# A normalised causal-attention layer on one NeuronCore: the store and the gather of the next batch's statistics registered one visit earlier

## The chip, the cores and the metric

The kernel runs on one core of one Trainium2 chip. A core has a matrix engine (PE, its weight loads shown as PEld), a vector engine (DVE), an activation engine (ACT), a general engine (POOL) and a sequencer (SP) that here only issues transfers. Each engine works through its own queue in order; between engines there are semaphores alone. The metric is the time of one execution on the device, in microseconds (us), lower is better. Times stand as the median of several runs; one more execution was taken with the profiler, and all views come from that one.

## The reference

The input x has 32 batches of 256 channels by 32x32 pixels (1024 tokens), in float32. Each batch is normalised in groups of eight channels, projected to queries, keys and values for eight heads of 32 channels, and put through attention in which a token sees only the tokens strictly before it; the result is added to x.

```python
g = x.reshape(B, 32, 8, H, W)                       # 32 groups of 8 channels
xn = (g - mean(g, axis=(2, 3, 4))) / sqrt(var(g, axis=(2, 3, 4)) + 1e-5)
q  = q_w @ xn + q_b;   k, v = split(kv_w @ xn + kv_b)
scores = q.T @ k / sqrt(32)                         # per head, 1024 x 1024
scores = where(mask == 0, -10000, scores)           # mask: strictly lower triangle
attn = where(mask == 0, 0, softmax(scores))
return x + attn @ v
```

## The kernel before

**Tiling.** Two groups of four heads (index g) and five blocks of keys and queries per group make ten *visits* per batch (N = 10, `VISITS`, line 692). In visit i the kernel forms scores on PE (`scores`, line 437) into the PSUM tiles `sT` and `tri`, takes exponentials on ACT (lines 473 and 476) into the tiles `e` and `eh`, and lets POOL zero what lies above the diagonal (`mask`, line 416, through `select`, line 411). One visit later PE multiplies the masked exponentials with the values (`values`, line 491, matmuls of line 502 into `acc`), ACT copies a finished `acc` into a tile `num` (line 511), and DVE adds exponentials up over keys (line 521), which gives the softmax's denominators. So PE, ACT, POOL and DVE work on neighbouring visits, and there are 320 visits in all.

**Order of the work.** It is written out by hand: `tc.manual_schedule` keeps every engine's instructions in the order in which Python emits them. The loop at line 881 goes through the visits; in visit i it emits, in this order, the scores, exponentials and masks of visit i; the first part of the products of visit i-1; whatever the table `at` holds for i; the second part of the products; DVE's additions of visit i-1, mixed with the chains in the table `beside`; and last whatever the table `after` holds for i. The function `when` (line 754) fills these tables, and tuples such as `PROJECT`, `PREPARE`, `SUMS`, `STACK`, `FINISH` give the visit of each step relative to the first visit of its batch (`first + n`).

**Statistics of a later batch.** `prepare` (line 757) registers twelve steps for batch b, at the visits `first + PREPARE[k]`:

- k = 0, 1: `norm_channels`, four `bn_stats` on DVE (line 195) that write the tile `st`, spread between DVE's additions.
- k = 2: `norm_gather`, one DMA issued by SP (line 207) that stores `st` (12 KB) to the DRAM tile `each`.
- k = 3: `norm_spread`, one indirect DMA issued by POOL (line 214) that reads `each` back so that every partition holds the numbers of all eight channels of its group, in the tile `eight`. It waits for the store.
- k = 4: `norm_groups`, two `bn_aggr` on DVE (line 223) from `eight` to `mv`, and two small operations (lines 224, 225).
- k = 5: `norm_rstd`, two operations on POOL (lines 252, 256): the power -0.5, and the shift.
- k = 6 to 11: `norm_apply`, which writes the normalised input `xn` on ACT (line 271) for the projections (line 179).

**What else stands around it.** On POOL: two transfers per denominator, which fold the sums `e` from 128 to 64 and from 64 to 32 rows (`fold`, line 550). On SP: the transfers `folded<-e` that put the four folded sums under each other (line 556), the store and the spread of the inverses (lines 616, 630: `rb<-inverses`), the outputs (line 662) and the input of two batches ahead (line 115). On DVE, for the batch two back: `num<-num,rb` (line 668) and `rb<-num,v_bias_col,x` (line 659), which is the last reader of a `num` tile, so that ACT may write it anew.

Of the kernel before, what the change touches and what calls it, by code (L numbers as in the profile page):

```python
# [33 lines left out]
def tile_norm_attention_residual(  # L34
# [69 lines left out]
    def unshifted():  # L104
# [652 lines left out]
        def prepare(b, whens):  # L757
            for n, f in zip(whens, [
                lambda: norm_channels(b, 0), lambda: norm_channels(b, 1), lambda: norm_gather(b), lambda: norm_spread(b),
                lambda: norm_groups(b), lambda: norm_rstd(b),  # L760
            ] + [lambda hf=hf, g=g: norm_apply(b, hf, g) for hf, g in ((0, 0), (0, 1))]
              + [lambda g=g, s=s: norm_apply(b, 1, g, (s,)) for g in range(NG) for s in range(2)]):
                if n is None:
                    in_turn([f() or []])
                elif isinstance(n, tuple):
                    n[1].setdefault(n[0], []).insert(len(beside.get(n[0], ())) if n[1] is beside else 0, f)
                else:
                    when(n, f, after)
# [8 lines left out]


        PROJECT = (-5, -4, -4, -3, -2, -1, 0, 1, 1, 2, 3, 4)
        PREPARE = (-13, -12, -10, -10, -9, -8, -7, -6, -5, -4, -4, -3)  # L780
        SUMS = (4, 6, 9, 11)
        STACK = (6, 9, 12, 14)
        LOAD = 5
# [5 lines left out]
        with tc.manual_schedule(engines={ENG.PE, ENG.Activation, ENG.DVE, ENG.Pool, ENG.SP}):  # L789
# [47 lines left out]
            for b in range(B):  # L837
# [4 lines left out]
                if b >= 2:  # L842
                    for n in range(NG * NH):
# [5 lines left out]
                    prepare(b, [  # L849
                        (first + n, {5: at}.get(k, beside)) if k in (0, 1, 4, 5) else first + n for k, n in enumerate(PREPARE)  # L850
                    ])
# [60 lines left out]
    def shifted():  # L912


        with ExitStack() as inner:
# [34 lines left out]
            with tc.For_i(0, B, 1) as b:  # L950
# [93 lines left out]
                )  # L1044

    inside = unshifted()
    ALL = 3 * P * ROW
    held = nc.values_load(
# [29 lines left out]
```

## Time and profile before

| what | value |
|---|---|
| median of the runs (lowest to highest) | 1793.87 us (1793.67 to 1795.77) |
| the profiled execution's own time | 1794.61 us |
| its span, first to last instruction | 1792.9 us |
| mean granted clock of PE over the span | 0.999 |
| busy: PE, DVE, ACT, POOL | 1763.3, 1598.2, 1450.1, 1195.0 us |
| busy share: PE, DVE, ACT, POOL | 98%, 89%, 81%, 67% |

The span is divided into 32 batches of some 55 us. "Busy" counts an engine's own instructions; issuing a DMA from SP, waits and branches are not counted. In a timeline a row gives the start (us from the span's start), the duration, engine, line, operation, output<-inputs, the count of merged instructions, and in brackets the idle time before the row with what ended it. In the list of waits a row gives who waited for what: total us, number of times, longest. In the chain of waits each row is one step of the chain that ended last, with its start and duration. A wait for several semaphores is put down to the one that came last.

### The profile page before, as it was taken

The numbers are of one execution on the slowest core, as the hardware profiler recorded it, in microseconds if no ns is written. First come the engines' busy times: TensorE is split into PE (matmuls) and PEld (weight loads), VectorE is DVE, ScalarE is ACT, GpSimd is POOL, SyncE is SP. The second block draws the span as 40 slices with busy tenths as digits, with TensorE's granted clock in tenths as the row PEclk, the third lists the DMA queues.
The fourth block names the chain that finished last, engine by engine and source line by source line (L and its number), as shares of the span: only waits on it lengthen the run. The fifth ranks groups of instructions, "written<-read, shape, count | busy, mean of one in ns | idle before, by whom it ended". The sixth has DMA issues, their size and how long they took to land.

```text
span 1792.9 us, 82114 instructions
## 1 busy us (share of the span) xinstructions
PE 1763.3 (98%) x37144; PEld 1074.1 (60%) x37144; DVE 1598.2 (89%) x1668; ACT 1450.1 (81%) x1736; POOL 1195.0 (67%) x1191
## 2 busy tenths in 40 slices
PE   9999999999999999999999999999999999999997
PEld 6666556556565565565655666656656656666564
DVE  4698888988889898898899999889999999999998
ACT  6888877888878877788888888778888888888885
POOL 2567766677666676666767667756677776677662
PEclk9999999999999999999999999999999999999999
DMA  2566767676666766667676677766777776767663
GB/s 69 99 121 142 145 123 139 141 142 138 131 144 133 140 137 135 138 136 146 137 141 129 138 147 141 145 120 138 149 141 140 144 131 135 150 142 145 131 127 89
DMA packets 92772, 240.23 MB, mean 134 GB/s; under 512 B 26272, under 2 KB 27792, under 8 KB 76544
## 3 DMA queue, kind: packets, MB, share of 16 engines
q0 software_dynamic: 17360, 100.58, 39.6%
q1 hardware_dynamic: 74912, 134.28, 26.3%
q8 instruction: 291, 4.77, 1.1%
q14 instruction: 65, 0.53, 0.1%
q10 hardware_dynamic: 144, 0.07, 0.0%
HBM read 69.90 MB, written 34.95 MB: 58 GB/s over the span
## 4 chain that ended last, share of the span: by engine, by line
PE 84%; DMA 6%; DVE 4%; ACT 3%; issue 1%; POOL 1%; SPq 0%; POOLq 0%; ACTq 0%; DVEq 0%
PE acc L502 25%; PE pp L179 21%; PE tri L404 13%; PE sT L404 13%; PE ppv L179 12%; DMA eight<-each,group_of 5%; DVE e L521 2%; ACT eh L476 1%; DVE rb L659 1%; ACT e L473 1%; ACT num L511 0%; POOL e L550 0%; DMA wn<-in_L_conv_kv_w_dram 0%; DMA rb<-inverses 0%; DMA folded<-e 0%
## 5 line engine op out<-in xcount | busy, mean ns | idle before, releaser
L473 ACT ACTIVATE e<-sT 128x1024 f32<-128x1024 f32 x640 | 621.1, 1023 | 198.5 <-PE sT L404 191.5
L404 PE MATMUL sT<-q,k 32*64 32x512 f32 (+3 forms) x6144 | 534.0, 522 | 0.0
L404 PE MATMUL tri<-q,k 32*64 32x64 f32 (+5 forms) x10752 | 522.7, 313 | 10.4 <-ACT eh L476 10.3
L404 PEld LDWEIGHTS tri<-q,k 32*64 32x64 f32 x10752 | 377.2, 130 | 191.7 <-issue 72.9
L179 PE MATMUL pp<-xn,wT 128*32 128x256 f32 x8192 | 490.8, 379 | 0.7 <-issue 0.7
L521 DVE TENSOR_TENSOR e<-e,eh 128x1536 f32<-128x1536 f32 x315 | 444.1, 1410 | 32.4 <-PE acc L502 24.5
L476 ACT ACTIVATE eh<-tri 128x1536 f32<-128x1536 f32 (+1 forms) x320 | 439.1, 1372 | 27.5 <-DVE e L521 18.1
L521 DVE TENSOR_TENSOR e<-e,e 128x2048 f32<-128x2048 f32 x189 | 453.7, 2400 | 3.3
L411 POOL TENSOR_SCALAR_AFFINE_SELECT diagonal<-eh 128x256 f32<-128x256 f32 (+1 forms) x384 | 400.4, 1218 | 21.2 <-ACT eh L476 17.7
L179 PEld LDWEIGHTS pp<-xn,wT 128*32 128x32 f32 x8192 | 262.6, 110 | 229.7 <-ACT e L473 61.9
L550 POOL DMA_DIRECT2D e<-e x248 | 256.3, 1034 | 182.2 <-DMA e<-e 103.7
L502 PE MATMUL acc<-e,v 128*32 128x512 f32 x2560 | 339.5, 600 | 8.3 <-ACT num L511 8.1
L404 PEld LDWEIGHTS sT<-q,k 32*64 32x64 f32 x6144 | 268.0, 131 | 8.4 <-ACT k L286 4.1
L179 PE MATMUL ppv<-wT,xn 128*32 128x256 f32 x4096 | 247.2, 381 | 0.3 <-issue 0.3
L502 PE MATMUL acc<-eh,v 128*32 128x384 f32 (+1 forms) x2560 | 199.9, 403 | 0.0
L411 POOL TENSOR_SCALAR_AFFINE_SELECT corner<-e 128x256 f32<-128x256 f32 x64 | 64.5, 1009 | 199.8 <-ACT e L473 199.8
L521 DVE TENSOR_TENSOR e<-e,diagonal 128x1024 f32<-128x1024 f32 x126 | 182.2, 1446 | 7.4 <-POOL corner L425 0.5
L179 PEld LDWEIGHTS ppv<-wT,xn 128*32 128x32 f32 x4096 | 126.6, 110 | 90.2 <-ACT e L473 16.5
L411 POOL TENSOR_SCALAR_AFFINE_SELECT e<-e 128x512 f32<-128x512 f32 x64 | 142.2, 2223 | 4.4
L223 DVE BATCH_NORM_AGGREGATE mv<-eight 128x2 f32<-128x96 f32 x62 | 35.9, 582 | 119.4 <-DMA eight<-each,group_of 119.4
L271 ACT ACTIVATE xn<-x,shift,rstd 128x256 f32<-128x256 f32 x248 | 138.6, 596 | 0.0
L502 PEld LDWEIGHTS acc<-eh,v 128*32 128x32 f32 x2560 | 76.6, 110 | 90.9 <-issue 64.0
(99 smaller groups left out, 1578.1 us busy)
## 6 DMA issues: line engine op xcount, KB each, us to landing
e<-e POOLq DMA_DIRECT2D x124, 512.0 KB, 6.0
x<-in_x_dram SPq DMA_DIRECT2D x124, 256.0 KB, 4.2
e<-e POOLq DMA_DIRECT2D x124, 256.0 KB, 4.8
folded<-e SPq DMA_DIRECT2D x124, 256.0 KB, 5.6
rb<-inverses SPq DMA_DIRECT2D x124, 256.0 KB, 4.0
out_dram<-rb SPq DMA_DIRECT2D x124, 256.0 KB, 5.3
x<-in_x_dram SPq DMA_DIRECT2D x2, 512.0 KB, 4.7
inverses<-inv_turned SPq DMA_DIRECT2D x31, 32.0 KB, 2.9
```

The source lines that it names most:

```text
L179: nc.tensor.matmul(out[part], lhsT=lhsT[:, part], rhs=rhs, start=start, stop=stop, skip_group_check=True)
L223: return [lambda g=g: nc.vector.bn_aggr(mv[:, g, :], live["eight", b][:, :, g, :]) for g in range(NG)] + [lambda: nc.vector.tensor_scalar( ...
L271: nc.scalar.activation(to, of, AF.Identity, bias=live["shift", b][:, g : g + 1], scale=rstd)
L404: return nc.tensor.matmul(to, lhsT=live["k", b, g][rows, kb * P + c : kb * P + c + KEYS], rhs=of, start=True, stop=True, skip_group_check=True
L411: nc.gpsimd.affine_select(out=to, in_=of, pattern=[[0, 4], [1, to.shape[-1]]], compare_op=ALU.is_gt, fill=0.0, base=first - (P - 1 if odd ...
L473: nc.scalar.activation(e[:, heads[a][0] : heads[a][1] + 1 : step, :], banks[a], AF.Exp)
L476: exp = nc.scalar.activation(eh[:, :, :wide], tri.rearrange("p (j q) -> p j q", q=SHORT)[:, :, :wide], AF.Exp)
L502: nc.tensor.matmul(acc[HD * j : HD * (j + 1), of], lhsT=live["v", b][:, kb, h * HD : (h + 1) * HD], rhs=e[:, j, :], start=first, stop=last ...
L521: nc.vector.tensor_add(to, to, tile_of(b, g, at))
L550: nc.gpsimd.dma_start(out=total[:rows], in_=total[rows : 2 * rows], accum_op=ALU.add)
L659: nc.vector.scalar_tensor_tensor(rb, num, v_bias_col[:, g : g + 1], xt[:, g, cols], ALU.add, ALU.add)
```

## The change

One number of the tuple `PREPARE` is changed twice: steps k = 2 (the store by SP) and k = 3 (the gather by POOL) of every batch from the third on are registered 11 instead of 10 visits before the batch's first visit. That is visit 9 of the batch two ahead of it, instead of visit 0 of the batch just ahead of it. Both steps stay in the table `after`, so they are emitted last in their visit.

```diff
         PROJECT = (-5, -4, -4, -3, -2, -1, 0, 1, 1, 2, 3, 4)
-        PREPARE = (-13, -12, -10, -10, -9, -8, -7, -6, -5, -4, -4, -3)
+        PREPARE = (-13, -12, -11, -11, -9, -8, -7, -6, -5, -4, -4, -3)
```

POOL's queue before, around visit 0 of batch 14. Names: `e_1_0` is the sum of group 1, first half of the queries, of batch 13; `corner`, `e_0_0`, `eh_0_0` are tiles of visit 0 of batch 14; `diagonal_0_1` of its visit 1; `eight` and `each` hold the statistics for batch 15.

```order
L550 DMA e_1_0_12082<-e_1_0_12082 64x2048
L411 AFFINE_SELECT corner_0_12558<-e_0_0_12520 128x4x64
L411 AFFINE_SELECT e_0_0_12520<-e_0_0_12520 128x4x128
L424 MEMSET e_0_0_12520 1x4
L425 COPY corner_0_12558<-eh_0_0_12521 64x4x64
L411 AFFINE_SELECT eh_0_0_12521<-eh_0_0_12521 128x4x128
L550 DMA e_1_0_12082<-e_1_0_12082 32x2048
L214 DMA eight_12611<-each_12609,group_of 128x192
L411 AFFINE_SELECT diagonal_0_1_12653<-eh_0_1_12614 128x4x128
L411 AFFINE_SELECT diagonal_0_1_12653<-eh_0_1_12614 128x4x64 x2
```

POOL's queue with the change, at the same place:

```order
L550 DMA e_1_0_12082<-e_1_0_12082 64x2048
L214 DMA eight_12522<-each_12520,group_of 128x192
L411 AFFINE_SELECT corner_0_12562<-e_0_0_12524 128x4x64
L411 AFFINE_SELECT e_0_0_12524<-e_0_0_12524 128x4x128
L424 MEMSET e_0_0_12524 1x4
L425 COPY corner_0_12562<-eh_0_0_12525 64x4x64
L411 AFFINE_SELECT eh_0_0_12525<-eh_0_0_12525 128x4x128
L550 DMA e_1_0_12082<-e_1_0_12082 32x2048
L411 AFFINE_SELECT diagonal_0_1_12653<-eh_0_1_12614 128x4x128
L411 AFFINE_SELECT diagonal_0_1_12653<-eh_0_1_12614 128x4x64 x2
```

The gather has moved ahead of six rows: the five operations that mask visit 0, and the second fold of `e_1_0`. It now stands behind the first fold of `e_1_0`.

SP's queue with the change, at the same place (`folded` gathers batch 13's sums, `rb` and `inverses` belong to batch 12):

```order
L616 DMA inverses_12338<-inv_turned_12336 128x2x32
L630 DMA rb_12424<-inverses_12338 32x4x512 x2
L556 DMA folded_12280<-e_0_1_11744 32x2048
L207 DMA each_12520<-st_12324 128x24
L630 DMA rb_12424<-inverses_12338 32x4x512 x2
L556 DMA folded_12280<-e_1_0_12082 32x2048
```

Apart from the number of a buffer these rows stood in this order before as well: between the ends of visits 9 and 0 SP issues nothing else, so the store keeps its place. The queues of PE, ACT and DVE are unchanged too.

## The prediction

> **What bounds the kernel now.** I read the batches' lengths first, by the busy time of the engines in stretches that run from the start of one visit 0's masks to a later one's (length, then busy time and instructions of PE, PEld, DVE, ACT, POOL, then PE's granted clock, DMA share, GB/s). They hold 11, 9 and 6 batches.
>
> ```profile
> 241.94:852.94 611.00, 600.09 (x12678) 363.97 (x12672) 552.84 (x573) 497.03 (x595) 417.54 (x407) 1.00 0.69 138
> 852.94:1348.58 495.64, 491.19 (x10376) 299.18 (x10368) 454.79 (x469) 407.06 (x487) 342.57 (x334) 1.00 0.70 139
> 1348.58:1675.38 326.80, 326.25 (x6919) 199.92 (x6912) 300.78 (x313) 271.62 (x325) 232.38 (x223) 1.00 0.70 140
> ```
>
> A batch takes 611.00/11 = 55.55 us in the first stretch, 55.07 in the second, 54.47 in the third. In the third PE is busy for 326.25 of 326.80 us: that is PE's own floor at full clock. In the first it idles 10.91 us, 0.99 per batch. So PE bounds the kernel, and what can be won is the distance from 54.47.
>
> What stops PE? The waits of the first stretch, then the one that matters in the third:
>
> ```profile
> DVE mv L223 <- DMA eight<-each,group_of: 45.8, 11, 4.7
> ACT num L511 <- DVE rb L659: 14.1, 11, 1.6
> ACT eh L476 <- DVE e L521: 10.8, 11, 1.0
> PE acc L502 <- ACT num L511: 7.0, 11, 1.0
> PE tri L404 <- ACT eh L476: 3.9, 11, 0.4
> DVE num L668 <- DMA rb<-inverses: 3.7, 8, 0.8
> ```
>
> ```profile
> DVE mv L223 <- DMA eight<-each,group_of: 20.8, 6, 3.6
> ```
>
> PE's two waits are 7.0 + 3.9 = 10.9 us, all that it idles. Each happens once per batch, and the chain of waits shows where both begin (batch 14):
>
> ```profile
> 805.84 5.16 DMA eight<-each,group_of
> ...
> 811.53 0.76 DVE rb L659
> ...
> 812.38 0.59 ACT num L511
> ...
> 813.94 1.77 DVE e L521
> ...
> 815.79 1.25 ACT eh L476
> ```
>
> The gather of the next statistics lands late, DVE stands at its `bn_aggr`, behind it in DVE's queue stands the `rb` operation for which ACT waits to overwrite `num`, and PE waits for ACT to empty `acc`; the late addition `e` holds the next exponential in the same way. DVE's wait is 4.16 us per batch in the first stretch and still 3.47 in the third, where PE loses nearly nothing: the first 3.5 us of it are covered by slack, and only the rest reaches PE, through two restarts. It need not vanish to be free.
>
> **What moves.** POOL's gather passes six POOL rows; nothing moves on SP, so the store leaves when it did. POOL before, in batch 14 (visit 0's masks from 797.48 to 804.78, the gather thereafter at 805.84):
>
> ```profile
> 793.96 0.85 POOL L550 DMA_DIRECT2D e<-e  x1 [1.79 <-PE pp L179]
> 797.48 1.23 POOL L411 TENSOR_SCALAR_AFFINE_SELECT corner<-e 128x256 f32<-128x256 f32 x1 [2.68 <-ACT e L473]
> 798.78 2.03 POOL L411 TENSOR_SCALAR_AFFINE_SELECT e<-e 128x512 f32<-128x512 f32 x1
> ...
> 803.27 1.51 POOL L411 TENSOR_SCALAR_AFFINE_SELECT eh<-eh 128x512 f32<-128x512 f32 x1
> ...
> 806.96 1.38 POOL L411 TENSOR_SCALAR_AFFINE_SELECT diagonal<-eh 128x512 f32<-128x512 f32 x3
> ```
>
> The store's row, the landing of all stores, the gather's duration on POOL and its landing (minimum, median, maximum; ns, then us):
>
> ```profile
> 794.94 0.34 SPq L207 DMA_DIRECT2D each<-st  x1
> ```
>
> ```profile
> DMA to landing us min/median/max: 1.7/5.3/6.1
> ```
>
> ```profile
> L214 POOL DMA_INDIRECT eight<-each,group_of x31: 1097/1312/1601, 17.3 to 1683.7; - x31
> ...
> DMA to landing us min/median/max: 2.9/5.1/5.7
> ```
>
> *When the gather goes.* POOL is ready for it at 794.81, the store lands at 794.94 + 5.3 = 800.2. So POOL now stands for 5.4 us at the gather, with the masks queued behind it. With the 0.3 us that POOL shows between a release and a gather (805.54 to 805.84) it starts at 800.5 and ends at 801.9; it lands at 800.5 + 5.1 = 805.6, instead of 811.0.
>
> *What DVE gains.* DVE's rows before:
>
> ```profile
> 803.05 1.23 DVE L521 TENSOR_TENSOR e<-e,diagonal 128x1024 f32<-128x1024 f32 x1
> ...
> 805.25 1.31 DVE L668 TENSOR_TENSOR num<-num,rb 128x512 f32<-128x512 f32 x2
> 811.03 0.59 DVE L223 BATCH_NORM_AGGREGATE mv<-eight 128x2 f32<-128x96 f32 x1 [4.46 <-DMA eight<-each,group_of]
> ```
>
> DVE reaches the `bn_aggr` at 805.25 + 1.31 = 806.6, one us after the new landing: no wait. Bounds: with store and gather both fastest it is the same; with both slowest (6.1, 1.6 and 5.7 us) the landing is at 807.0 and the wait 0.4, far under the 3.5 that are free. The `rb` operation then ends some 4.4 us sooner; ACT needs 1.2 of that, and the next exponential 1.0.
>
> *What the masks lose.* They start at 801.9 instead of 797.48, 4.4 us late. PE reads them here (first row: masked `e`, then `eh`, then the diagonals of visit 1; the last is today's stall):
>
> ```profile
> 804.88 1.04 PE L502 MATMUL acc<-e,v 128*32 128x512 f32 x8
> 807.60 1.07 PE L502 MATMUL acc<-eh,v 128*32 128x384 f32 x16
> 810.22 0.62 PE L502 MATMUL acc<-diagonal,v 128*32 128x128 f32 x16
> 813.01 1.07 PE L502 MATMUL acc<-e,v 128*32 128x512 f32 x8 [0.57 <-ACT num L511]
> ```
>
> At their durations of today (7.3 us in all, `e` ready after 3.4) `e` would come at 805.3, `eh` at 809.2: PE late by 0.4 and 1.6 us. But a mask's duration is not fixed. Batch 0 shows the same masks while DVE idles:
>
> ```profile
> 23.90 0.42 POOL L411 TENSOR_SCALAR_AFFINE_SELECT corner<-e 128x256 f32<-128x256 f32 x1 [5.35 <-ACT e L473]
> 24.39 0.64 POOL L411 TENSOR_SCALAR_AFFINE_SELECT e<-e 128x512 f32<-128x512 f32 x1
> ...
> 25.23 0.39 POOL L425 COPY corner<-eh 64x256 f32<-64x256 f32 x1
> 25.69 0.64 POOL L411 TENSOR_SCALAR_AFFINE_SELECT eh<-eh 128x512 f32<-128x512 f32 x1
> ```
>
> From 23.90 to 26.33 that is 2.4 us in all. And batch 14's three diagonals took 1.38 us at 806.96, in DVE's wait, against 3.47 us under DVE's additions:
>
> ```profile
> 832.70 3.47 POOL L411 TENSOR_SCALAR_AFFINE_SELECT diagonal<-eh 128x512 f32<-128x512 f32 x3
> ```
>
> The Trainium skill, "SBUF — State Buffer", section "Who interferes with whom", has the rule: a DVE instruction with two SBUF inputs and a GpSimd (POOL) instruction that reads SBUF need the same port, and the one that comes second blocks until the first is done. DVE's additions are of that kind, so by the rule this change pushes the masks against whatever DVE does from 801.9 on; were those additions as dense as at 797 to 804, the sum would end as in the slow rival below. The pairs 2.4 and 7.3, 1.38 and 3.47, bear the rule out.
>
> So it matters where DVE is from 801.9 on. Freed of its wait, it runs ahead of today's times until other data stop it. The lead is at least 0 and at most the 4.46 won. Its nearest stop that I see is the last `folded` transfer, at 822.19, which lands a median 5.6 us later, 827.8, while DVE reads it at 830.78:
>
> ```profile
> 822.19 0.51 SPq L556 DMA_DIRECT2D folded<-e  x1
> ```
>
> ```profile
> 830.78 0.70 DVE L564 STREAM_TRANSPOSE turned<-folded 128x512 f32<-128x512 f32 x1
> ```
>
> That leaves up to 3.0; I take 2. Then the last addition ends at 803.05 + 1.23 - 2 = 802.3, a few small operations follow until about 803, and DVE must stand until 805.2 for the `rb` loads: SP issues them behind a wait for PE, so they do not move (DVE waits for them in 8 of 11 batches already). The masks thus have DVE's additions beside them for 0.4 us and then a nearly idle DVE: between 2.4 and some 3.5 us, ready by 805.4 at the latest, `e` by 804. PE's 804.88 and 807.60 are met. The second fold follows at 805.4 (804.7 today), the diagonals from 806.3; even at 3.47 us they end at 809.8, ahead of 810.22.
>
> What was behind the gather in POOL's queue (diagonals, folds, the power -0.5) is no longer behind it, and the power no longer waits for DVE.
>
> **The sum.** Batches at 54.47 us: 11 x 1.08 = 11.9 us from the first stretch, 9 x 0.60 = 5.4 from the second, nothing from the third. In the second there is a gap of PE with no known cause, which I leave in (0.7):
>
> ```profile
> 1174.11 0.40 PE L179 MATMUL pp<-xn,wT 128*32 128x256 f32 x1 [0.68 <-issue]
> ```
>
> The first batches and the end stay. 11.9 + 5.4 - 0.7 = 16.6 us. The profiled execution took 1794.61 us in all, so 1778.0; it was 0.7 above the median of the runs, which is within what a run varies, so I forecast 1778 us.
>
> **Rivals.**
>
> *The masks come too late (slower).* If DVE is not ahead, its additions lie beside the masks, and they take today's 7.3 us. The point from which it decides: `eh` must be masked by 807.60, 5.7 us after 801.9. At 7.3 us PE stands 1.6 us in each of some 30 batches, 48 us, against 16.6 won: 1794.6 + 48 - 16.6 = 1826 us. With the diagonals at 3.47 us on top it is up to 3 us per batch, 1868. For it: POOL really stands 5.4 us with the masks behind it. Against: removing DVE's wait is what puts DVE ahead, and each stall of PE puts it further ahead. Chance 0.15.
>
> *The stall changes its name (no change).* The gather now runs together with the `rb` loads. If these came 3.5 us later, DVE would stand at `num<-num,rb` for what it stood at `bn_aggr`, and `rb` would be no sooner: 1794 us. For it: DVE waits there already, 3.7 us in 11 batches. Against: the gather lands in 5.1 us beside a 512 KB fold today. Chance 0.10, with whatever else would eat the gain.
>
> *The change does less than it says.* Half of it is void: the store does not move, and that is in the sum. If the gather landed as late as today, nothing would be left; but it is issued 5 us sooner.
>
> **Numbers.** The forecast has 0.75; its own range is 1773 (the third stretch's last 0.1 per batch, and a second run's level) to 1786 (half the batches keep their stall). To leave out no more than 2 in 10 the range takes in the no-change rival, to 1798. A measurement of this kernel tells about 0.2% (3.6 us) from no change: faster 0.75, same 0.10, slower 0.15.
>
> **What would show it.** Right: DVE's wait at `bn_aggr` under 1 us per batch; its wait at `num<-num,rb` grown to some 2 us; POOL's gather waiting about 5 us for `each<-st`; visit 0's masks shorter than 7.3 us; PE busy for over 99% of batches 4 to 29. Wrong: PE waiting for POOL's `eh`, `e` or `diagonal`; a landing of the gather after 810; the `rb` loads later than 806.

## The result and the profile after

The changed kernel takes 1776.14 us (median of 6 runs, 1773.88 to 1779.02) beside 1793.77 us for the kernel before (6 runs, 1789.89 to 1795.77): a ratio of 0.9904 (95% interval 0.9890 to 0.9919), 17.6 us saved. The forecast was 1778. Two later comparisons of the same pair, each beside its own runs of the kernel before, gave 1769.75 us (expected at 1776 again) and 1771.69 us, ratios of 0.9868 (0.9849 to 0.9886) and 0.9873 (0.9855 to 0.9891). So the gain is 1.0 to 1.3%, and the first figure is at its lower end.

The batches first, in the changed kernel's profile: stretches of again 11, 9 and 6 batches, from the start of one visit 0's masks to that of a later one (length, then busy time and instructions of PE, PEld, DVE, ACT, POOL, then PE's clock, DMA share, GB/s).

```profile
245.96:843.83 597.87, 597.87 (x12700) 368.02 (x12697) 554.38 (x572) 498.07 (x596) 368.39 (x408) 1.00 0.70 141
843.83:1335.74 491.91, 490.75 (x10380) 302.84 (x10376) 454.43 (x468) 407.60 (x487) 302.73 (x333) 1.00 0.71 140
1335.74:1663.27 327.53, 327.51 (x6912) 201.84 (x6908) 303.39 (x312) 270.90 (x325) 199.03 (x223) 1.00 0.71 140
```

A batch now takes 54.35, 54.66 and 54.59 us, where it took 55.55, 55.07 and 54.47. PE, which idled for 10.91 us in the first stretch, idles for none of it. Of the 17.8 us by which the span shrank (1792.9 to 1775.1) the first stretch gives 611.00 - 597.87 = 13.1 and the second 495.64 - 491.91 = 3.7; the third gives 0.7 back, and the remaining 1.7 lie ahead of these stretches and behind them.

The waits of that first stretch:

```profile
POOL eight L214 <- DMA each<-st: 49.2, 9, 6.8
...
DVE num L668 <- DMA rb<-inverses: 35.2, 11, 4.6
```

DVE's wait for `eight` (45.8 us in 11 batches before) has no row any more, and neither have ACT's two waits for DVE and PE's two for ACT. In their place stand POOL at the gather, 5.5 us in each of nine batches, and DVE at the `rb` loads, 3.2 us per batch in place of 0.3. Both are new or larger, and PE waits for neither. (In the other two batches of the stretch the profile puts POOL's wait down to an addition on DVE, 8.4 us in all; there too the gather starts 0.3 us after the store has landed, as it does in every batch of this run.)

The order of one batch (12) in the timeline, PE, DVE, POOL and SP:

```profile
672.18 0.85 POOL L550 DMA_DIRECT2D e<-e  x1 [1.05 <-PE pp L179]
...
672.85 0.53 SPq L207 DMA_DIRECT2D each<-st  x1
...
678.28 1.23 DVE L521 TENSOR_TENSOR e<-e,diagonal 128x1024 f32<-128x1024 f32 x1
...
679.47 1.15 POOL L214 DMA_INDIRECT eight<-each,group_of  x1 [6.44 <-DMA each<-st]
...
680.63 0.44 POOL L411 TENSOR_SCALAR_AFFINE_SELECT corner<-e 128x256 f32<-128x256 f32 x1
...
681.83 0.10 POOL L424 MEMSET e<- 1x4 f32 x1
...
682.33 0.64 POOL L411 TENSOR_SCALAR_AFFINE_SELECT eh<-eh 128x512 f32<-128x512 f32 x1
...
684.40 1.50 DVE L668 TENSOR_TENSOR num<-num,rb 128x512 f32<-128x512 f32 x2 [4.49 <-DMA rb<-inverses]
...
685.82 0.57 DVE L223 BATCH_NORM_AGGREGATE mv<-eight 128x2 f32<-128x96 f32 x1
```

```profile
683.12 0.59 PE L502 MATMUL acc<-e,v 128*32 128x512 f32 x1
...
686.09 1.07 PE L502 MATMUL acc<-eh,v 128*32 128x384 f32 x16
```

POOL stands 6.44 us for the store. The masks run from 680.63 to 682.97, 2.34 us in all, since DVE's last addition ended at 679.51 and DVE, but for two short operations, stands until 684.40 for `rb`. The masked `e` is there at 681.93 and PE reads it at 683.12: a margin of 1.2 us. `eh` has 3.1. DVE reaches its `bn_aggr` without a wait. In this batch that is the picture of the prediction, step for step.

### The profile page after: what moved, and what is told of

Its sections match the earlier page's. It is cut to its first block, busy times and chain, and to the rows that moved or that the text cites. A ratio compares the mean times of both kernels' runs of the same rounds, so it can differ in the third digit from the quotient of the medians.

```text
span 1775.1 us, 82114 instructions
## 1 busy us (share of the span) xinstructions
PE 1761.9 (99%) x37144; PEld 1085.2 (61%) x37144; DVE 1598.8 (90%) x1668; ACT 1450.3 (82%) x1736; POOL 1053.2 (59%) x1191
## 4 chain that ended last, share of the span: by engine, by line
PE 96%; DVE 1%; DMA 1%; issue 0%; POOL 0%; SPq 0%; DVEq 0%; ACT 0%; POOLq 0%; ACTq 0%
PE acc L502 29%; PE pp L179 25%; PE tri L404 15%; PE sT L404 14%; PE ppv L179 13%; DVE e L521 0%; DMA rb<-inverses 0%; DMA wn<-in_L_conv_kv_w_dram 0%; DMA e<-e 0%; DMA x<-in_x_dram 0%; DMA folded<-e 0%; DVE num L668 0%; DVE rb L659 0%; DVE turned L564 0%; DVE rows L567 0%
## 5 line engine op out<-in xcount | busy, mean ns | idle before, releaser
L179 PE MATMUL pp<-xn,wT 128*32 128x256 f32 x8192 | 494.0, 379 | 0.0
L179 PEld LDWEIGHTS pp<-xn,wT 128*32 128x32 f32 x8192 | 268.9, 110 | 222.7 <-ACT e L473 60.5
L411 POOL TENSOR_SCALAR_AFFINE_SELECT diagonal<-eh 128x256 f32<-128x256 f32 (+1 forms) x384 | 369.1, 1110 | 24.7 <-ACT eh L476 23.2
L550 POOL DMA_DIRECT2D e<-e x248 | 222.1, 896 | 209.1 <-DMA e<-e 101.2
L502 PE MATMUL acc<-e,v 128*32 128x512 f32 x2560 | 343.5, 600 | 0.0
L179 PE MATMUL ppv<-wT,xn 128*32 128x256 f32 x4096 | 252.2, 381 | 1.2 <-issue 1.1
L668 DVE TENSOR_TENSOR num<-num,rb 128x512 f32<-128x512 f32 x124 | 116.5, 960 | 99.0 <-DMA rb<-inverses 99.0
L179 PEld LDWEIGHTS ppv<-wT,xn 128*32 128x32 f32 x4096 | 129.6, 109 | 92.3 <-ACT e L473 18.3
L521 DVE TENSOR_TENSOR e<-e,diagonal 128x1024 f32<-128x1024 f32 x126 | 165.3, 1312 | 7.4 <-DVE e L521 0.9
L214 POOL DMA_INDIRECT eight<-each,group_of x31 | 49.9, 1608 | 166.8 <-DMA each<-st 135.1
L411 POOL TENSOR_SCALAR_AFFINE_SELECT corner<-e 128x256 f32<-128x256 f32 x64 | 56.0, 875 | 146.1 <-ACT e L473 145.7
L411 POOL TENSOR_SCALAR_AFFINE_SELECT corner<-eh 128x256 f32<-128x256 f32 x64 | 60.1, 940 | 132.3 <-ACT eh L476 132.3
```

The costliest lines, as they stand in the source:

```text
L179: nc.tensor.matmul(out[part], lhsT=lhsT[:, part], rhs=rhs, start=start, stop=stop, skip_group_check=True)
L214: nc.gpsimd.indirect_dma_start(eight, None, live["each", b].rearrange("(m c) s -> m (c s)", c=CPG), bass.IndirectOffsetOnAxis(ap=group_of[ ...
L411: nc.gpsimd.affine_select(out=to, in_=of, pattern=[[0, 4], [1, to.shape[-1]]], compare_op=ALU.is_gt, fill=0.0, base=first - (P - 1 if odd ...
L502: nc.tensor.matmul(acc[HD * j : HD * (j + 1), of], lhsT=live["v", b][:, kb, h * HD : (h + 1) * HD], rhs=e[:, j, :], start=first, stop=last ...
L521: nc.vector.tensor_add(to, to, tile_of(b, g, at))
L550: nc.gpsimd.dma_start(out=total[:rows], in_=total[rows : 2 * rows], accum_op=ALU.add)
```

## The experiments

The first four edit the kernel before. The program's `when` puts a step at the end of a visit (table `after`); "behind the fold" and the like speak of POOL's queue around visit 0.

**The store alone.** Only step k = 2 moves; the gather stays in visit 0.

```diff
-        PREPARE = (-13, -12, -10, -10, -9, -8, -7, -6, -5, -4, -4, -3)
+        PREPARE = (-13, -12, -11, -10, -9, -8, -7, -6, -5, -4, -4, -3)
```

> Only the store is registered a visit earlier, the gather stays at visit 0. The queue of every engine reads as before. My theory: 1794 us, no change, ratio 0.998 to 1.002. Rival (the store itself gains): under 1790 us.

Measured: 1794.01 us beside 1793.57, ratio 1.0001 (0.9989 to 1.0013). The store's half of the edit does nothing by itself; all of the gain is the gather's.

**The gather behind the masks.** With the store as above, the gather is put at the head of visit 0's `after`: behind the five masks, but ahead of the second fold.

```diff
-                        (first + n, {5: at}.get(k, beside)) if k in (0, 1, 4, 5) else first + n for k, n in enumerate(PREPARE)
+                        (first + n, {3: after, 5: at}.get(k, beside)) if k in (0, 1, 3, 4, 5) else first + n for k, n in enumerate(PREPARE)
```

> The gather goes only a little sooner than before: behind the five masks of visit 0, ahead of the second fold of the sum; the store stays. So POOL never stands with masks behind it, and the gather leaves about 1.1 us sooner than before (the fold's 0.81 us and the 0.3 us of issue). My theory (the first 3.5 us of DVE's wait at bn_aggr are free): the wait falls from 4.2 to about 3.1 us per batch, PE's two stalls are gone, 1776 to 1782 us, ratio to before 0.990 to 0.993. Rival (the gain goes with the wait removed): 1.1 of 4.2 us of the wait gives a quarter of 17.6 us, about 1789 us, ratio 0.9975. Rival (the gain came from the masks, which POOL now does beside an idle DVE): 1794 us, no change.

Measured: 1768.75 us (1766.59 to 1770.61), ratio 0.9858 (0.9841 to 0.9876). The gather passes one row, the 256 KB fold, and gains all that the change gains, and more. Its group of instructions, and how long it took from its start to its landing:

```profile
L214 POOL DMA_INDIRECT eight<-each,group_of x31: 1102/1107/1270, 17.3 to 1654.2; - x31
...
DMA to landing us min/median/max: 2.6/2.7/4.5
```

```profile
DVE mv L223 <- DMA eight<-each,group_of: 9.6, 3, 5.2
```

```profile
240.30:836.13 595.83, 595.83 (x12679) 364.07 (x12672) 563.77 (x573) 497.50 (x595) 398.82 (x407) 1.00 0.71 141
836.13:1323.63 487.50, 487.50 (x10376) 297.90 (x10368) 460.36 (x469) 407.04 (x487) 329.11 (x333) 1.00 0.71 141
1323.63:1648.63 325.00, 325.00 (x6919) 198.60 (x6912) 308.80 (x313) 271.39 (x325) 216.96 (x222) 1.00 0.71 141
```

The landing takes 2.7 us in place of 5.1, DVE's wait falls from 119.4 us to 9.6, and a batch takes 595.83/11 = 54.17 us in the first stretch, 487.50/9 = 54.17 in the second and 325.00/6 = 54.17 in the third. Single batches agree too: from each one's first `ppv` weight load to the next one's, batches 4 to 30 all take 54.17 us. I had expected DVE to keep about 3 us of its wait per batch; it kept none in these stretches, because I had moved the time of issue only and left the landing at 5.1 us.

**The gather still later.** Two fills of a 128x512 tile on POOL ahead of the gather of the kernel before, behind the fold.

```diff
+            for _ in range(2 if b > 1 else 0):
+                nc.gpsimd.memset(spare, 0.0)
             live["eight", b] = eight.rearrange("p (c g s) -> p c g s", c=CPG, g=NG)
```

> The kernel before, with two memsets of a spare tile (128x512) on POOL just ahead of the gather, about 1.1 us in all, so that the statistics land that much later and nothing else moves. My theory: past the free 3.5 us each microsecond of DVE's wait reaches PE, 1.1 us in each of 30 batches, some 33 us: about 1827 us, ratio 1.015 to 1.02, with PE's waits for num and for eh doubled. Rival (DVE's wait is a symptom, the landing of the gather does not set the time): 1794 us, no change.

Measured: 1800.44 us, ratio 1.0029 (1.0019 to 1.0040): a small loss, far from the theory's number. The second fold of batch 14 in the kernel before, and then the same place with the fills:

```profile
804.73 0.81 POOL L550 DMA_DIRECT2D e<-e  x1
```

```profile
805.71 0.81 POOL L554 DMA_DIRECT2D e<-e  x1
...
806.23 1.42 POOL L216 MEMSET spare<- 128x512 f32 x2
807.82 1.10 POOL L218 DMA_INDIRECT eight<-each,group_of  x1 [0.16 <-issue]
```

```profile
DMA to landing us min/median/max: 2.8/4.1/5.1
```

```profile
DVE mv L227 <- DMA eight<-each,group_of: 119.5, 31, 8.9
```

The gather starts 2.1 us behind the fold instead of 1.1, and lands in 4.1 us instead of 5.1: its landing hardly moves against the fold's, and DVE waits what it did. Together with the run above this says that the landing is set by the fold that was issued ahead of it, more than by the gather's own issue. A fold of 256 KB lands a median 4.8 us after its start in the kernel before:

```profile
e<-e POOLq DMA_DIRECT2D x124, 256.0 KB, 4.8
```

In batch 14 of the kernel before this fold landed 4.7 us after its start, at 809.4, and the gather at 811.0. With the fills the fold landed at 805.71 + 4.6 = 810.3, and the gather at 807.82 + 4.3 = 812.1. So it came 1.6 and 1.8 us behind the fold. That distance isn't fixed: from batch 4 on it lies between 0.2 and 2.1 us in both runs, with medians of 1.3 and 1.6, but the gather never lands ahead of the fold.

**`bn_aggr` behind the `rb` operations.** In the kernel before, DVE does its `rb` operations of visit 0 first and waits for `eight` after them; nothing else moves.

```diff
+                elif n == "behind":
+                    when((b - 1) * N + 1, lambda f=f: in_turn([f()]), after)
...
-                        (first + n, {5: at}.get(k, beside)) if k in (0, 1, 4, 5) else first + n for k, n in enumerate(PREPARE)
+                        "behind" if k == 4 else (first + n, {5: at}.get(k, beside)) if k in (0, 1, 4, 5) else first + n for k, n in enumerate(PREPARE)
```

> The kernel before, with the two bn_aggr put behind the two rb operations in DVE's queue; POOL and SP as before, so the gather lands as late as before. This tells PE's two stalls apart. My theory: the rb operations no longer stand behind the late gather, so ACT's wait for num and PE's 7.0 us per 11 batches at acc go; the late addition behind bn_aggr still holds the next exponential, so the 3.9 us per 11 batches at tri stay, and by the same share 60 to 65% of the gain comes: about 1783 us, ratio 0.993 to 0.995. Rival (it is only the sum of DVE's waits that counts, not what stands behind them): DVE's wait shrinks by the 1.5 us of the rb operations, a third of it, 1788 us. Rival (the masks' contention is what counts): 1794 us.

Measured: 1779.24 us, ratio 0.9915 (0.9900 to 0.9929).

```profile
DVE mv L223 <- DMA eight<-each,group_of: 40.4, 29, 6.8
...
ACT eh L476 <- DVE e L521: 4.6, 8, 1.0
```

ACT's wait for `rb` (20.1 us before) is gone, and the run wins 14.3 of the 24.8 us that the kernel with the gather behind the masks wins. What is left of DVE's wait, 1.4 us per batch, still holds some additions, and ACT's `eh` eight times for them. But hardly any of that reaches PE: between 240 and 1665 us PE waits 0.5 us for `eh` where it waited 7.2 before, and for `num` not at all where it waited 7.6. So the chain that the prediction read from the waits (gather, `bn_aggr`, `rb`, ACT, PE) is confirmed, and my theory that the second wait (`tri` for `eh`) would stay was wrong: it went as well. What keeps this run 10.5 us behind the other is not explained by them; the largest row of PE there is a pause with no named cause (`PE ppv L179 <- issue`, 5.5 us in four pauses), in the slowest of the six runs, 1785.07 us.

The next four edit the changed kernel.

**Additions in DVE's gap.** Four two-input additions of 128x512 behind line 601, where DVE stands for `rb`.

```diff
+                for _ in range(4 if b < B - 2 else 0):
+                    nc.vector.tensor_add(spare, wT[:, 0, :HALF], wT[:, 1, :HALF])
```

> The changed kernel with four additions of two SBUF tiles (128x512, some 0.6 us each, 2.5 us in all, into a spare tile that nobody reads) on DVE just ahead of num<-num,rb, in the stretch where DVE stands for the rb loads (3.2 us per batch) and POOL masks visit 0. DVE's own end does not move. My theory (the masks are short because DVE's two-input additions no longer lie beside them): the masks grow from 2.3 us to 4.5 us or more, e comes up to 2 us later than now, where PE has a median of 1.35 us to spare, and PE stands about 0.5 to 1.5 us per batch: 1785 to 1820 us. Rival (the masks are short for another reason, such as POOL having no fold beside them, or their length does not matter): 1776 us.

**One-input statistics in the same gap.** The same place, with an operation of nearly the same length that reads one operand.

```diff
+                for _ in range(4 if b < B - 2 else 0):
+                    nc.vector.bn_stats(spare[:, :6], wT[:, 0, :HALF])
```

> The same place and the same length on DVE, but four bn_stats of one SBUF tile (128x512, some 0.6 us each, into a spare tile that nobody reads): one SBUF input instead of two. My theory (it is the second input, not that DVE is busy): the masks stay at 2.3 us and the time at 1776 us, ratio to before 0.989 to 0.993. Rival (any busy DVE slows POOL): as with the additions, 1785 to 1820 us.

Measured, on one chip with the changed kernel at 1769.75 us: 1794.26 (ratio to before 1.0009, 0.9998 to 1.0021) with the additions, 1769.58 (0.9866, 0.9849 to 0.9882) with the statistics. DVE and POOL with the additions:

```profile
685.27 2.29 DVE L523 TENSOR_TENSOR e<-e,e 128x2048 f32<-128x2048 f32 x1
686.22 1.62 POOL L413 TENSOR_SCALAR_AFFINE_SELECT corner<-e 128x256 f32<-128x256 f32 x1
...
688.02 1.60 DVE L523 TENSOR_TENSOR e<-e,diagonal 128x1024 f32<-128x1024 f32 x1 [0.46 <-POOL corner L413]
...
690.57 3.70 DVE L605 TENSOR_TENSOR spare<-wT 128x512 f32<-128x512 f32 x4
```

With the statistics:

```profile
679.67 2.87 DVE L605 BATCH_NORM_STATS2 spare<-wT 128x6 f32<-128x512 f32 x4
680.35 0.44 POOL L413 TENSOR_SCALAR_AFFINE_SELECT corner<-e 128x256 f32<-128x256 f32 x1
680.85 0.64 POOL L413 TENSOR_SCALAR_AFFINE_SELECT e<-e 128x512 f32<-128x512 f32 x1
```

Beside `bn_stats` the masks are as short as beside an idle DVE (0.44 and 0.64 us): that DVE is busy doesn't stretch them, and the statistics cost nothing. The additions cost 24.5 us, and by another way than meant. They take 3.70 us where the statistics take 2.87, DVE loses its lead, and so its own additions (the rows at 685.27 and 688.02) lie beside the masks again, of which the first now takes 1.62 us; the added ones come behind the masks here, and in most batches beside the last of them or behind it. PE then waits both for the masks and for ACT, which waits for `rb` as in the kernel before:

```profile
PE tri L406 <- ACT eh L478: 12.9, 21, 1.8
...
ACT num L513 <- DVE rb L663: 11.2, 18, 0.7
...
PEld acc L504 <- POOL e L426: 6.9, 18, 0.9
```

The two can't be divided in this run, so it does not price the masks. What it shows is that four additions in the gap undo nearly all that the change won, where four `bn_stats` in the same place undo nothing.

**POOL held up ahead of the gather.** Four fills ahead of the gather, meant to delay the masks.

```diff
+            for _ in range(4 if b > 1 else 0):
+                nc.gpsimd.memset(spare, 0.0)
             live["eight", b] = eight.rearrange("p (c g s) -> p c g s", c=CPG, g=NG)
```

> The changed kernel with four memsets of a spare tile (128x512, about 2.1 us in all) on POOL ahead of the gather. If POOL runs them while it would wait for the store anyway they cost nothing: POOL waits some 5 us there. My theory: 1776 us, ratio 0.989 to 0.993, the wait for the store shorter by 2.1 us. Rival (POOL's instructions ahead of visit 0's masks are on the path): up to 2.1 us per batch less the 1.35 us that PE has to spare, 20 us or more: 1796 us.

Measured: 1770.20 us, ratio 0.9866 (0.9849 to 0.9883), no different from the changed kernel beside it.

```profile
POOL eight L218 <- DMA each<-st: 47.9, 14, 7.4
```

The fills did not delay the masks: they lie in the time in which POOL stands for the store, whose wait, by this row, fell from 105.3 us in the changed kernel beside it to 47.9. POOL's standing there is idle time that other work of POOL could use, some 2.6 us of it at no cost.

**POOL held up behind the gather.** The same four fills between the gather and the masks, so that the masks are truly late.

```diff
             )
+            for _ in range(4 if b > 1 else 0):
+                nc.gpsimd.memset(spare, 0.0)
```

> The changed kernel with four fills of a 128x512 tile on POOL (some 2.7 us together) between the gather and visit 0's masks: the masks really start 2.7 us later, and nothing else is added. Theory (the masks have a margin of little more than a microsecond: in the changed kernel the masked e stands a median 1.35 us ahead of PE's read of it): PE waits for POOL's e some 1.3 us in most batches, batches of 55.5 to 56 us, 1800 to 1815 us. Rival (the masks' time does not matter here, their cover is larger than it looks, or the rest of the loop absorbs a one-off shift): 1770 to 1780 us with PE busy over 99%.

Measured: 1810.14 us (1808.00 to 1814.08), ratio 1.0083 (1.0061 to 1.0104), beside 1771.69 for the changed kernel on that chip: 38.5 us lost. PE and POOL in batch 8:

```profile
469.68 1.87 POOL L216 DMA_INDIRECT eight<-each,group_of  x1 [6.25 <-DMA each<-st]
...
471.55 2.29 POOL L221 MEMSET spare<- 128x512 f32 x4
...
474.98 0.10 POOL L428 MEMSET e<- 1x4 f32 x1
...
...
475.13 1.06 PE L506 MATMUL acc<-e,v 128*32 128x512 f32 x8 [1.42 <-POOL e L428]
```

```profile
PE acc L506 <- POOL e L428: 21.4, 18, 2.5
```

PE takes the masked `e` 0.05 us after POOL has finished it. This is the slow rival, brought about by the fills: 2.3 us more on POOL between the gather and the masks cost 1.3 us per batch on average, and put the kernel above the one before. PE's waits for `e` by name are 21.4 of the 38.5 us, in 18 batches; the rest has no such row. The mechanism was real, and the changed kernel stands about a microsecond away from it: `e` is there a median 1.2 us ahead of PE's read in batches 4 to 30 of its first profile, and 0.13 us at the least.

**Late, but ahead of the fold.** In the kernel with the gather behind the masks, three fills ahead of the gather, which is then issued nearly as late as in the kernel before, still ahead of the fold.

```diff
+            for _ in range(3 if b > 1 else 0):
+                nc.gpsimd.memset(spare, 0.0)
             live["eight", b] = eight.rearrange("p (c g s) -> p c g s", c=CPG, g=NG)
```

> The kernel with the gather behind visit 0's masks but ahead of the second fold, with three fills (some 2 us) between the masks and the gather: the gather is issued nearly as late as in the kernel before, but not behind the fold. Theory (it is the fold queued ahead that makes the gather land late): it lands 2.7 us after its start, DVE's wait at bn_aggr stays at or below 1.5 us a batch, PE has no stall, 1767 to 1774 us. Rival (the time of issue alone counts): DVE's wait is back at 3 to 4 us a batch and the time at 1788 to 1796 us.

Measured: 1778.85 us (1776.57 to 1782.88), ratio 0.9912 (0.9890 to 0.9933): between the two theories. The landing is as the first one has it, 3.0 us:

```profile
DMA to landing us min/median/max: 2.6/3.0/4.2
```

DVE's wait is not: it was to stay under 1.5 us. The two halves of this run differ, which makes it useful. DVE's waits from 230 to 900 us and from 900 to 1640 us, with 12 of them each, and the batches' lengths (batches 4 to 16, and 16 to 29):

```profile
DVE mv L227 <- DMA eight<-each,group_of: 33.8, 12, 3.4
...
DVE mv L227 <- DMA eight<-each,group_of: 19.5, 12, 2.3
```

```profile
244.04:898.87 654.83, 652.75 (x13832) 396.93 (x13824) 607.67 (x625) 542.75 (x649) 465.10 (x481) 1.00 0.69 140
898.87:1603.30 704.43, 704.43 (x14982) 431.35 (x14976) 655.83 (x678) 587.85 (x703) 512.99 (x520) 1.00 0.70 141
```

With 2.8 us of waiting per wait a batch takes 654.83/12 = 54.57 us, with 1.6 it takes 704.43/13 = 54.19. So 1.6 us of DVE's wait cost next to nothing. That the first half's 0.40 us per batch are the price of the longer wait is not shown: PE's two waits of the kernel before, for `num` and for `eh`, have no row in this stretch, and of the 2.1 us that PE idles there 0.9 are a pause at `pp` with no named cause, 0.7 a wait for ACT's `v`, and 0.2 one for POOL's diagonals, which stand behind the fills. Of the 11 us between this run and the kernel without the fills (1767.92 on that chip) 12 x 0.40 = 4.8 are the first half's; some 3 lie in the first 100 us, where the granted clock of the profiled run was 0.97 and that of the kernel without the fills 1.00.

**The two best, side by side.** No edit: the changed kernel, and the one with the gather behind the masks, on one chip.

> The changed kernel once more, beside the kernel with the gather behind the masks on the same chip. If the exposed wait for the store and the thin margin of the masks cost anything, it is slower than that kernel by 0.1 to 0.4%, at 1768 to 1777 us; if both only reach PE's floor, the two agree within 0.1%.

> The kernel with the gather behind visit 0's masks and ahead of the second fold, once more. Both theories: 1766 to 1770 us; what is compared is its distance from the changed kernel run beside it.

Measured: 1771.69 us (1768.85 to 1774.89) and 1767.92 us (1766.76 to 1770.62), ratios to before of 0.9873 (0.9855 to 0.9891) and 0.9848 (0.9831 to 0.9866). The second is 3.8 us or 0.2% ahead. The intervals overlap, so this alone doesn't settle it; its earlier 1768.75 lies below all three medians of the changed kernel as well. The profiles say the same batch by batch (first `ppv` weight load to the next, batches 4 to 30): the second kernel stays at 54.17 to 54.28 us in both its profiles, while of the changed kernel's 27 batches 14 took more than 54.20 us in its first profile, and 5 in each of the later two, up to 55.75. It has the same gather ahead of the same fold and neither the stand for the store nor the thin margin, so where a choice is to be made, it is the better of the two.

## Why the prediction was right, and where it was not

*What bounds the kernel* was right, and so was the chain from the gather to PE: putting `bn_aggr` behind `rb` gives 14.3 us and takes away both of PE's waits but for 0.5 us. *The sum* came out at 16.6 against 17.6 measured in the first comparison, 23.2 and 23.6 in the others. The term that was off is **the floor**: I took the third stretch's 54.47 us per batch for PE's own, since PE was busy for 326.25 of 326.80 us. The kernel with the gather behind the masks takes 54.17. A busy share of 100% was no floor: the changed kernel's third stretch has PE busy for 327.51 of 327.53 us at 54.59 us a batch. 26 batches at 0.30 us are 7.8 us, which would have made the sum 24.4, what that kernel gains (24.8). By the same error the first 3.5 us of DVE's wait were called free: in the stretch from which that was read, a batch took 0.30 us more than the floor. That 1.6 us are nearly free the second half of the run with the gather late but ahead of the fold shows (54.19 us); where the price begins was not settled.

That 16.6 came so near 17.6 is luck in part. The forecast had 11.9, 4.7 and 0 us for the three stretches and nothing for the rest; the profile gives 13.1, 3.7, -0.7 and 1.7. A floor taken 0.3 us too high stood in for 0.2 to 0.5 us per batch by which the changed kernel's first profile stays above the true one. Most of that excess is no wait by name, but part is a pause of the kind that the prediction had left in as 0.7 us of unknown cause:

```profile
PE ppv L179 <- issue: 1.1, 2, 0.8
```

Why the first comparison came out 4 to 6 us above the later two was not settled; its profile has 14 batches above 54.20 us where theirs have 5.

*When the gather goes*: forecast 5.4 us of standing at the store, 5.6 measured (135.1 us in the 24 batches that the profile puts down to the store; 5.4 over all 31). *Its landing* was taken at 5.1 us from its start and measured at 4.4. The 5.1 was the right row read the wrong way: it held the rest of a fold issued 1.1 us earlier. The 4.4 is more than the 2.7 that the gather takes behind the masks: here SP issues the two `rb` loads at nearly the same moment (678.88 against 679.47 in batch 12, where the gather landed in 4.6), and in batches 9 and 27, where they come more than 2 us later, it landed in 3.0 and 2.7. The misreading did no harm, as the bound had room, but it hid that passing this one row was enough. The prediction also called that fold 512 KB; it is the second one, of 256.

*The masks* were the step with most at risk: forecast 2.4 to 3.5 us in place of 7.3, measured 2.34 in batch 12, which is also the median of batches 4 to 30; in 5 of these 27 they took over 4 us. The prediction argued it from the Trainium skill, "SBUF — State Buffer", section "Who interferes with whom". The run with statistics in DVE's gap agrees with that section's other half as well, by which a DVE instruction with at most one SBUF input (outside certain faster modes) does not contend: four `bn_stats` left the masks at 0.44 and 0.64 us.

The batch in which the prediction was worked, 14, turned out otherwise, and shows why the margin holds. There the store landed early:

```profile
780.10 0.53 SPq L207 DMA_DIRECT2D each<-st  x1
...
780.81 0.85 POOL L550 DMA_DIRECT2D e<-e  x1 [1.40 <-PE pp L179]
...
783.18 1.10 POOL L214 DMA_INDIRECT eight<-each,group_of  x1 [1.52 <-DMA each<-st]
...
784.35 1.05 POOL L411 TENSOR_SCALAR_AFFINE_SELECT corner<-e 128x256 f32<-128x256 f32 x1
...
785.47 2.57 POOL L411 TENSOR_SCALAR_AFFINE_SELECT e<-e 128x512 f32<-128x512 f32 x1
...
789.44 0.63 POOL L411 TENSOR_SCALAR_AFFINE_SELECT eh<-eh 128x512 f32<-128x512 f32 x1
```

The masks start while DVE still adds, and take 5.7 us; but they start early, and end at 790.07, ahead of PE's reads (`e` at 791.76, `eh` at 794.43). When the store is late they are late and short. The two sizes lean against each other.

*DVE's lead and the wait at `rb`*: forecast some 2 us, measured 3.2 per batch (35.2 in 11). The rival in which *the stall changes its name* has its sign there, and no price: the time before was lost because `rb` came after the wait at `bn_aggr`, and now `bn_aggr` comes after the wait at `rb`.

*The masks too late*: the mechanism is there, as the fills behind the gather show. Two of its details were off. I had it decide at `eh`, by 807.60; what PE waits for is `e`, which has 1.2 us in batch 12 where `eh` has 3.1. And the price is 38.5 us for 2.3 us of delay, less than each delayed microsecond reaching PE in each of 30 batches (69), as the masks have that margin first.

## What to carry to other kernels

A small transfer's time to landing can include a large one that was issued ahead of it, in its own queue or by another engine: before moving a small late transfer a whole stage, look for the one large transfer it stands behind. An engine's busy share doesn't give its floor; the shortest stage that any variant reaches is the better guide, above all when all its batches agree. When a step is pushed later, ask what its neighbours do at its new time: here the masks became three times shorter in most batches, because the additions beside them had gone.

## What was not expected of the hardware

- A gather issued behind a 256 KB fold on POOL landed a median 5.1 us after its start when it was issued 1.1 us after the fold, and 4.1 when it was issued 2.1 us after it, each time behind the fold; ahead of the fold it took 2.7. The Trainium skill, "DMA: Bandwidth & Descriptors", section "Two DMAs through the same engine are not ordered", says that within one queue of one DMA engine descriptors start in order, which fits; that this kernel's gather pays the fold ahead for it is only seen here.
- The store of 12 KB took a median 5.9 us to land in the changed kernel. In batch 12 it landed 6.3 us after its issue at 672.85, in batch 14 2.8 us after 780.10. SP had issued a transfer of 256 KB 0.6 us ahead of it both times (672.24 and 779.49), so this one isn't what makes the difference. The 512 KB fold of POOL differs: issued at 672.18 in batch 12, ahead of the store, and at 780.81 in batch 14, behind it. From batch 2 on, 22 stores had such a fold issued 0.3 to 2 us ahead and landed in 5.3 to 6.6 us, a median 0.2 us after the fold did; four had none in the 5 us ahead and landed in 2.7 to 4.1; the three with the fold less than 0.3 us ahead lie between, at 3.9 to 4.5. So by these traces POOL, standing for the store, stands for the most part for its own fold, though another engine issued the store. No run moved the store ahead of the fold to try it.

```profile
each<-st SPq DMA_DIRECT2D x31, 12.0 KB, 5.9
```
